# The last convolution's products: half of the row pairs as 64x32, half as pairs of 32x32 spread over two steps, with loads in small pieces

## The chip, the cores and the metric

The kernel runs on one core of one Trainium2 chip, in one launch. The metric is the device time in microseconds; shown are the median and the range of three runs, and one further execution taken with the profiler, from which all rows and durations come. Names: PE is TensorE (matmuls), PEld its weight loads, DVE VectorE, ACT ScalarE, POOL GpSimd, SP SyncE, which only issues transfers.

## What is computed

The reference is a chain of four layers on an image batch `x` of shape 8 x 16 x 256 x 256 (images, channels, rows, columns), all in float32. Each layer normalises its input by groups of two channels and adds its own result to it. The change lies in the last layer. Written with Fourier transforms, it is in effect a 3x3 convolution over 16 channels whose edges wrap around:

```python
def _gn(v, G=8, eps=1e-5):
    B_, C_, H_, W_ = v.shape
    g = v.reshape(B_, G, C_ // G, H_, W_)
    m = jnp.mean(g, axis=(2, 3, 4), keepdims=True)
    s = jnp.var(g, axis=(2, 3, 4), keepdims=True)
    return ((g - m) / jnp.sqrt(s + eps)).reshape(v.shape)

def _L3_conv_ref(x, weight):
    ...
    w_pad = _circular_pad(weight, H, W, k, p)
    dL = jnp.asarray(np.outer(_diag_L(H, k), _diag_L(W, k)))
    Lw = jnp.fft.fft2(w_pad * dL)
    Kx = jnp.fft.ifft2(x, norm='ortho')
    z = jnp.einsum('oihw,bihw->bohw', Lw, Kx)
    y = jnp.fft.fft2(z, norm='ortho')
    return jnp.real(y).astype(x.dtype)

x = x + _L0_conv_ref(_gn(x), L0_conv_weights)
x = x + _L1_conv_ref(_gn(x), ...)
x = x + _L2_conv_ref(_gn(x), ...)
x = x + _L3_conv_ref(_gn(x), L3_conv_weight)
```

## The kernel before

The four layers run one after the other. The last one, `layer3`, starts when layer 2 has written its result to `x3` in device memory, with one column of padding on each side (`WP` = 258 columns).

An image stands in SBUF as a tile of 128 partitions x 33 groups x 258 columns. The 256 rows are cut so that a partition holds one of 8 row positions and one of 16 channels: eight consecutive rows are four "row groups" of two rows, each on 32 partitions. Group index g steps by eight rows. The first image lies in `x30` (named `pt` in the profile, as it shares layer 2's buffer), the others in two tiles `x3s`; three buffers take turns.

An output of two rows x 16 channels, 32 results, needs four input rows, that is two neighbouring row groups of 32 partitions. `products` makes the first half of that sum with q = 0 and the second with q = 1. For each of three column offsets `dw` it issues, for four row pairs j and four column blocks c of the array, a product of a 32 x 32 weight with 512 columns (two groups of 256); so 16 products of 32 rows and 32 columns stand in different cells of the 128 x 128 array. Each product is two matmul instructions in the profile (float32 is made in two passes), each with its own weight load.

A step s = 0 to 3 of an image makes, for each column block c, the 16 output rows of groups 8c + 2s and 8c + 2s + 1: 64 rows. Two steps form a pair and share an output tile `y3` (four buffers). Within a pair the order is: q = 0 of both steps, then q = 1 of both. In PSUM each step has two tiles of two banks; there are four such tiles in all[...]. Between q = 0 and q = 1 a small copy (`seen`, line 1585) reads one column of the banks, by ScalarE for the first step and by VectorE for the second, so that the second half starts only when the first is complete. After q = 1, `evict` adds the bias and writes to `y3`: ScalarE (line 1537) for the even step, VectorE (line 1535) for the odd one, two instructions each. `store` (line 1545) writes the pair with 16 transfers, half on SP's queue and half on POOL's.

Loads: `fetch3` brings an image with two transfers of 16 groups and one of the last group. In `layer3` they are issued by ScalarE: images 1 and 2 at the start, image n + 2 in the middle of image n. `weights` (line 1502) scales the weights by the image's normalisation on VectorE. The normalisation of the last image isn't known when the stage starts; its statistics, a chain of small steps on several engines, are put between the pairs one by one (`todo`).

The order within an engine is the order of the code, since the stage runs under a manual schedule. Earlier, layer 1 (line 1006) uses products of 128 x 32 and of 64 x 32.

Of the kernel before, what the change touches and what calls it, by code (L numbers as in the profile page):

```python
# [10 lines left out]
F32 = mybir.dt.float32  # L11
AF = mybir.ActivationFunctionType
ALU = mybir.AluOpType
# [4 lines left out]
B, C, H, W = 8, 16, 256, 256  # L18
# [96 lines left out]

def _turned(a):

    return np.concatenate([a.reshape(P, 3 * 2 * 32), a[..., ::-1].reshape(P, 3 * 2 * 32)], 1)


def _embedding():
# [162 lines left out]
class _Net:  # L284
# [950 lines left out]
    def stats3_steps(self, pool, name, bank):  # L1235

        nc = self.nc
        mv = self.st3[1]
        e, own, dg, out, nm, bias = (
            pool.tile([P, n], F32, name=f"{name}_{k}")  # L1240
            for k, n in dict(e3=P, own=2, dg=16, bc=16, nm=8, bias=8).items()
        )
        dg, out = dg.rearrange("p (i b) -> p i b", i=2), out.rearrange("p (i b) -> p i b", i=2)
        p, q, u, z = bank(), bank(), bank(), bank()
        (m, r), steps = self.norm_steps(pool, name, bank, self.k["pair"], own[:, 0:1], own[:, 1:2])

        def about():

            nc.vector.tensor_tensor(e, mv[:, 0], p()[:, :P], ALU.subtract)
            nc.vector.tensor_tensor(e, e, e, ALU.mult)  # L1250
            nc.vector.tensor_tensor(e, e, mv[:, 1], ALU.add)

        def columns():
            for i, a in enumerate((mv[:, 0], e)):
                nc.tensor.matmul(q()[:, i : i + 1], a, self.k["mean"][:, 0:1], start=True, stop=True)  # L1255

        def turn():
            nc.vector.tensor_scalar(dg[:, 0], self.k["hi8"], m, None, ALU.mult)
            nc.vector.tensor_scalar(dg[:, 1], self.k["hi8"], r, None, ALU.mult)

        def shift():

            nc.vector.tensor_copy(out, u()[:, :16].rearrange("p (i b) -> p i b", i=2))
            nc.vector.tensor_tensor(nm, out[:, 0], out[:, 1], ALU.mult)
            nc.vector.tensor_scalar(nm, nm, -1.0, None, ALU.mult)

        def sums():

            for q in range(4):
                at = slice(32 * q, 32 * q + 32)  # L1270
                for k in range(6):
                    nc.tensor.matmul(  # L1272
                        z()[at, :8], self.w3[at, 0, k // 2, k % 2], nm[at], start=k == 0, stop=k == 5
                    )
# [34 lines left out]
    def early3(self, pool):  # L1309

        self.st3 = pool.tile([P, P, 6], F32, name="st3"), pool.tile([P, 2, P], F32, name="mv3")
        self.nc.vector.memset(self.st3[1], 0.0)
        self.w3 = pool.tile([P, 2, 3, 2, 32], F32, name="w3")
        self.nc.sync.dma_start(out=self.w3.rearrange("p f d t m -> p (f d t m)"), in_=self.d["l3"])
        self.small = pool

    def patch(self, b, half, c, n):
# [77 lines left out]

    def first3(self, b):

        self.fetch3(self.nc.sync, b, self.x30.rearrange("p (g w) -> p g w", w=WP))

    def stats3(self, bank, name):  # L1400
        out, steps = self.stats3_steps(self.small, name, bank)
# [61 lines left out]

    def fetch3(self, engine, b, xs):

        rows = self.x3[b].rearrange("r c h k w -> (r c) (h k w)")
        at = xs.rearrange("p g w -> p (g w)")
        for k in range(0, 32 * WP, 16 * WP):  # L1470
            engine.dma_start(out=at[:, k : k + 16 * WP], in_=rows[:, k : k + 16 * WP])
        engine.dma_start(out=at[:32, 32 * WP :], in_=rows[:32, :WP])

    def layer3(self, images=range(B)):

# [5 lines left out]
        with ExitStack() as st:  # L1481
# [11 lines left out]

                return get

            def fetch(b, xs):
                self.fetch3(nc.scalar, b, xs)
                return xs

            def weights(b):  # L1500
                ws = io.tile([P, 2, 3, 2, 32], F32, name="ws3")
                nc.vector.scalar_tensor_tensor(  # L1502
                    ws.rearrange("p f d t m -> p (f d t m)"),
                    self.w3.rearrange("p f d t m -> p (f d t m)"),
                    stat[b][0][:, 1, b : b + 1],
                    self.k["ident3"],
                    ALU.mult,
                    ALU.add,
                )
                return ws  # L1510

            def products(s, q, ws, xs, ps):

                for dw in range(3):
                    for j in range(4):
                        k = (j + q) % 4
                        for c in range(4):
                            g = 8 * c + 2 * s + (j + q) // 4
                            nc.tensor.matmul(  # L1519
                                ps[j // 2][32 * c : 32 * c + 32, j % 2].rearrange("p (g w) -> p g w", w=W),  # L1520
                                ws[32 * k : 32 * k + 32, j % 2, dw, q],
                                xs[32 * k : 32 * k + 32, g : g + 2, dw : dw + W],
                                start=q == 0 and dw == 0,
                                stop=q == 1 and dw == 2,
                                skip_group_check=True,
                            )

            def evict(b, s, ps, y):

                bias = stat[b][1][:, b : b + 1]  # L1530
                for k in range(2):
                    src = ps[k].rearrange("p j (g w) -> p g j w", w=W)
                    to = y[:, s % 2, :, 2 * k : 2 * k + 2]
                    if s % 2:
                        nc.vector.tensor_scalar(to, src, bias, None, ALU.add)  # L1535
                    else:
                        nc.scalar.activation(to, src, AF.Identity, bias=bias)  # L1537

            def store(b, s, y):

# [20 lines left out]
                        put(0, [[W, 1], [1, W]], y[0, :, c, 15:16])  # L1561

            images = list(images)
            seen = [io.tile([P, 2, 2], F32, name=f"seen{k}", bufs=1) for k in range(2)]
            xs = [self.x30.rearrange("p (g w) -> p g w", w=WP)]
            ws = weights(images[0])

            stat[images[-1]], todo = self.stats3_steps(self.small, "g3b", bank)
            with tc.manual_schedule():
                for b in images[1:3]:  # L1570
                    xs.append(fetch(b, io.tile([P, 33, WP], F32, name="x3s")))
                for n, b in enumerate(images):
                    for s in (0, 2):
                        y = io.tile([P, 2, 2, 4, W], F32, name="y3", bufs=4)
                        if s and n and n + 2 < len(images):
                            xs.append(fetch(images[n + 2], xs[n - 1]))
                        ps = [[psum.tile([P, 2, 512], F32, name="p3") for _ in range(2)] for _ in range(2)]
                        for q in range(2):
                            for k in range(2):
                                products(s + k, q, ws, xs[n], ps[k])  # L1580
                                if q:
                                    evict(b, s + k, ps[k], y)
                                else:
                                    for h in range(2):
                                        (nc.vector.tensor_copy if k else nc.scalar.copy)(
                                            seen[k][:, h], ps[k][h][:, :, 0]
                                        )
                        store(b, s, y)
                        if todo:
                            todo.pop(0)[2]()  # L1590
                        while todo and todo[0][0] != "PE":
                            todo.pop(0)[2]()
                        if s == 0 and n + 1 < len(images):
                            ws_after = weights(images[n + 1])
                    if n + 1 < len(images):
                        ws = ws_after


@with_exitstack
# [66 lines left out]
```

## Time and profile before

| what | value |
|---|---|
| median of 3 runs | 6728.88 us (6724.0 to 6730.53) |
| the profiled execution's own time | 6725.06 us |
| its span, first to last instruction | 6723.2 us |
| mean granted TensorE clock | 0.985 |
| PE busy over the span | 6116.5 us (91%) |
| last convolution, first to last matmul (line 1519) | about 6444.6 to 6706.9 us from the start |
| of the whole span, matmul records of line 1519 | 6144 of 46024 |

A row of the profile that describes a group of instructions reads: line, engine, operation, output <- inputs by the program's names, shapes, count | busy us, mean ns of one | idle time of the engine just before them, and what ended it. "Issue" there is time in which an engine waited for nothing that the profile shows. A table by stretches gives, for each stretch in us from the start, busy time and count for each engine, then the granted clock, the share of time in which the 16 DMA engines were busy, and what they moved in GB/s. In a timeline the first two numbers are the start and the length in us. A line of a DMA view gives queue and kind, packets, MB and the share of 16 engines' time.

### The profile page before, as it was taken

Reading aid. Unit: us, or ns where it says so; the run is one execution under the profiler, and the core shown is the slowest. Engines: PE = TensorE matmul, PEld = TensorE weight load, DVE = VectorE, ACT = ScalarE, POOL = GpSimd, SP = SyncE. Lnnn points to the kernel's source line nnn. Section 1 sums busy time; section 2 is a strip of 40 time slices with the busy share of each in tenths; the row PEclk is TensorE's granted clock in tenths of the full one; section 3 lists DMA queues with packets and bytes.
Section 4 is the critical chain, followed back from the end, with each engine's and each line's share of the span. In section 5 each row is a group of like instructions: output and inputs, shape, how many; then the busy total and the mean of one; then the engine's idle time right before and its main releaser. Section 6 shows DMA issues by size and latency. Waiting matters only on the chain. (4 is left out here: it accounts for less than half of the span.)

```text
span 6723.2 us, 111466 instructions
## 1 busy us (share of the span) xinstructions
PE 6116.5 (91%) x46024; PEld 2770.6 (41%) x46024; DVE 5401.4 (80%) x6374; ACT 2738.3 (41%) x3898; POOL 3275.4 (49%) x2181
## 2 busy tenths in 40 slices
PE   3898998899899998998997799999999999999987
PEld 1333333333333333333332344444444566666654
DVE  5799999999999999999998899999999633333321
ACT  1333333333333333333332688888888421111211
POOL 0566666666666666666667333444343211111112
PEclk9999999999999999999997899999999999999999
DMA  6233333333333333333332555555556633344256
GB/s 260 61 87 91 92 91 93 88 88 94 90 90 89 88 88 88 88 88 88 88 89 60 180 176 176 175 173 178 176 175 178 174 93 80 80 102 97 81 181 213
DMA packets 372111, 800.86 MB, mean 119 GB/s; under 512 B 56210, under 2 KB 189842, under 8 KB 334354
## 3 DMA queue, kind: packets, MB, share of 16 engines
q1 hardware_dynamic: 329058, 713.30, 36.9%
q10 hardware_dynamic: 36144, 63.64, 2.6%
q0 software_dynamic: 6400, 16.78, 0.9%
q8 instruction: 361, 5.91, 0.4%
q14 instruction: 148, 1.21, 0.1%
HBM read 582.87 MB, written 210.77 MB: 118 GB/s over the span
## 5 line engine op out<-in xcount | busy, mean ns | idle before, releaser
L750 POOL TENSOR_TENSOR dd<-dd 128x1024 f32<-128x1024 f32 x512 | 1214.2, 2372 | 614.8 <-DVE dd L741 594.7
L1006 PE MATMUL ps<-bases,tw 128*32 128x512 f32 (+1 forms) x13824 | 1361.5, 545 | 16.9 <-POOL bases L975 6.5
L741 DVE SCALAR_TENSOR_TENSOR dd<-rb,v 128x1024 f32<-128x1024 f32 (+1 forms) x1024 | 1066.7, 1083 | 97.9 <-PE rb L730 90.2
L975 POOL TENSOR_TENSOR bases<-e,a 128x1024 f32<-128x1024 f32 (+1 forms) x264 | 621.8, 2379 | 928.3 <-DVE e L973 928.0
L629 DVE TENSOR_TENSOR pr<-v,fb 128x2048 f32<-128x2048 f32 (+1 forms) x512 | 1011.5, 2017 | 24.0 <-PE pl L639 12.8
L523 PE MATMUL cv<-kt,w 128*128 128x512 f32 x2048 | 1003.4, 612 | 27.4 <-DVE dd L741 21.4
L532 ACT COPY v<-cv 128x1024 f32<-128x1024 f32 x512 | 517.3, 1010 | 1154.2 <-PE cv L527 1154.2
L1006 PEld LDWEIGHTS ps<-bases,tw 128*32 128x32 f32 x13824 | 599.0, 109 | 800.8 <-issue 483.2
L750 POOL TENSOR_TENSOR s<-s,dd 128x512 f32<-128x512 f32 x512 | 671.3, 1311 | 35.1
L730 PE MATMUL rb<-rs,ct_fold 32*128 32x512 f32 x3584 | 608.7, 649 | 72.1 <-ACT rs L712 68.0
L750 POOL TENSOR_TENSOR s<-v,dd 128x512 f32<-128x512 f32 x256 | 330.7, 1292 | 660.0 <-DVE dd L741 660.0
L639 PE MATMUL pl<-pr,ct_fold 128*32 128x512 f32 x3584 | 532.5, 607 | 117.4 <-DVE pr L629 117.4
L527 PE MATMUL cv<-kt,w 64*128 64x512 f32 x2048 | 578.8, 641 | 0.0
L523 PEld LDWEIGHTS cv<-kt,w 128*128 128x128 f32 x2048 | 354.9, 191 | 524.7 <-issue 299.8
L1430 ACT ACTIVATE vt<-pv,w_b2v 128x128 f32<-128x128 f32 x512 | 146.5, 368 | 842.3 <-PE pv L1426 842.3
L1419 PE MATMUL pqk<-w_qk,t 128*128 128x512 f32 x1024 | 482.7, 594 | 4.6 <-POOL t L1413 4.6
L1451 DVE TENSOR_TENSOR y<-po,res 128x512 f32<-128x512 f32 x128 | 88.5, 692 | 490.9 <-PE po L1446 471.9
L983 DVE SCALAR_TENSOR_TENSOR bases<-xr,xm,bases 128x1024 f32<-128x1024 f32 (+1 forms) x264 | 447.8, 1734 | 0.3 <-POOL bases L975 0.3
L1413 POOL TENSOR_TENSOR t<-t,emb 128x512 f32<-128x512 f32 x128 | 162.3, 1268 | 507.1 <-DVE t L1409 496.4
L960 ACT ACTIVATE sq<-a 128x1024 f32<-128x1024 f32 (+1 forms) x264 | 263.8, 999 | 230.1 <-DVE a L952 229.3
L730 PEld LDWEIGHTS rb<-rs,ct_fold 32*128 32x128 f32 x3584 | 172.8, 185 | 416.3 <-issue 217.7
L942 ACT ACTIVATE d<-xr,bd,sd 128x1024 f32<-128x1024 f32 (+1 forms) x264 | 319.1, 1209 | 14.4 <-DMA xr<-x1p 14.4
(258 smaller groups left out, 8419.4 us busy)
## 6 DMA issues: line engine op xcount, KB each, us to landing
kt<-d SPq DMA_DIRECT2D x256, 516.0 KB
xr<-x1p SPq DMA_DIRECT2D x120, 1024.0 KB
d<-dn ACTq DMA_DIRECT2D x64, 516.0 KB
x<-y SPq DMA_DIRECT2D x128, 258.0 KB
xs<-in_x_dram SPq DMA_DIRECT2D x16, 2048.0 KB
xs<-in_x_dram SPq DMA_DIRECT2D x64, 512.0 KB
res<-in_x_dram SPq DMA_DIRECT2D x64, 512.0 KB
x<-s SPq DMA_DIRECT2D x128, 256.0 KB
```

Source lines behind the costliest of these rows:

```text
L523: nc.tensor.matmul(ps()[:, n], w[:, 0, j, :], t[:, a : a + 2, 0:W], start=True, stop=False)
L527: nc.tensor.matmul(ps()[:, n], w[at, 1, j, :], t[at, a : a + 2, 2 - n : 2 - n + W], start=False, stop=True)
L532: nc.scalar.copy(v[h]()[:, 4 * g : 4 * g + 4, j * W : j * W + W], ps().rearrange("p n (a w) -> p (n a) w", w=W),)
L629: nc.vector.tensor_tensor(pr()[:, :n].rearrange("p n (r w) -> p n r w", w=W), v[h]()[:, 4 * g : 4 * g + n].rearrange("p n (r w) -> p n r w ...
L639: nc.tensor.matmul(pl()[at : at + 32], sel[:, g, h, :], pr()[:, t, :], start=h == 0 and g == 0, stop=h == 1 and (g == 1 or t == 3),)
L730: nc.tensor.matmul(r()[:, n], spread[at, g, h, :], rs()[at], start=True, stop=True)
L741: nc.vector.scalar_tensor_tensor(dd()[:, :n], r()[:, :n], 1.0 / B, v[h]()[:, a : a + n], ALU.subtract, ALU.mult)
L750: op("POOL", us, lambda: nc.gpsimd.tensor_tensor(out[0](), a[0](), b[0](), ALU.add), a[1] + b[1], out[1])
L975: nc.gpsimd.tensor_tensor(ring[n % 3][:, 0, p : p + m, 1 : 1 + W], rows(e), rows(a), ALU.subtract)
L983: nc.vector.scalar_tensor_tensor(r, rows(part[1]), xm[:, b : b + 1], v, ALU.is_gt, ALU.mult)
L1006: nc.tensor.matmul(out if k is None else out[:, k], lhs, rhs, start=start, stop=stop, skip_group_check=True)
L1419: nc.tensor.matmul(ps, t[:, n, k * P : (k + 1) * P], wqk[:, n, :], start=n == 0, stop=n == 1)
```

## The change

- Even row pairs (`whole`): the two row groups of output pair j = 0 or 2 are neighbours that start at partition 0 or 64, so both halves of the sum are made at once, as one product with a 64 x 32 weight. A step has 3 x 2 x 4 = 24 of them.
- Odd row pairs (`halves`): as before in two halves of 32 x 32. The q = 0 half of a step is issued together with the q = 1 half of the step before it; the two use different rows of the array and different PSUM tiles. A step has 2 x 24 = 48 of them, and a last call after the loop makes the last q = 1 half.
- PSUM: a step has one tile for its even and one for its odd pairs. The even tile is evicted by ScalarE in its own step, the odd one by VectorE in the next. The stores of a pair of steps are issued one step later than the pair's end. One `seen` copy a step, by ScalarE.
- Loads: nine transfers an image (eight of four groups, one of the last group), on SP and POOL in turn, behind the stores of these queues: image 1 at the start, and image n + 2 in two portions, after steps 1 and 3 of image n.
- The weights are laid out anew: 96 columns for the 64-row products and 192 for the halves, 288 for 384.

```diff
+    both = np.concatenate([np.stack([a[2 * h + q, :, :, :, q] for q in range(2)]) for h in range(2)])
+    return np.concatenate([both.reshape(P, 3 * 32), a[..., ::-1].reshape(P, 3 * 2 * 32)], 1)
...
-    def fetch3(self, engine, b, xs):
+    def fetch3(self, engines, b, xs, part=range(9)):
 
         rows = self.x3[b].rearrange("r c h k w -> (r c) (h k w)")
         at = xs.rearrange("p g w -> p (g w)")
-        for k in range(0, 32 * WP, 16 * WP):
-            engine.dma_start(out=at[:, k : k + 16 * WP], in_=rows[:, k : k + 16 * WP])
-        engine.dma_start(out=at[:32, 32 * WP :], in_=rows[:32, :WP])
+        n = 4 * WP
+        for i in part:
+            engine = engines[i % len(engines)]
+            if i < 8:
+                engine.dma_start(out=at[:, i * n : (i + 1) * n], in_=rows[:, i * n : (i + 1) * n])
+            else:
+                engine.dma_start(out=at[:32, 32 * WP :], in_=rows[:32, :WP])
...
+            def product(ps, j, c, rows, w, xs, g, dw, start, stop):
+                nc.tensor.matmul(
+                    ps[32 * c : 32 * c + 32, j].rearrange("p (g w) -> p g w", w=W),
+                    w[rows],
+                    xs[rows, g : g + 2, dw : dw + W],
...
+            def whole(s, ws, xs, ps):
 
                 for dw in range(3):
-                    for j in range(4):
-                        k = (j + q) % 4
+                    for j in range(2):
                         for c in range(4):
...
+                            rows = slice(64 * j, 64 * j + 64)
+                            product(ps, j, c, rows, ws[0][:, dw], xs, 8 * c + 2 * s, dw, dw == 0, dw == 2)
+
+            def halves(work):
+
+                for dw in range(3):
+                    for q, s, ws, xs, ps in work:
+                        for j in range(2):
+                            k = (2 * j + 1 + q) % 4
+                            rows = slice(32 * k, 32 * k + 32)
+                            for c in range(4):
+                                g = 8 * c + 2 * s + (2 * j + 1 + q) // 4
+                                product(
+                                    ps, j, c, rows, ws[1][:, dw, q], xs, g, dw, q == 0 and dw == 0, q == 1 and dw == 2
+                                )
+
+            def evict(b, s, j, ps, y):
...
+                to = y[:, s % 2, :, j::2]
+                if j:
+                    nc.vector.tensor_scalar(to, src, bias, None, ALU.add)
+                else:
+                    nc.scalar.activation(to, src, AF.Identity, bias=bias)
...
+                    full, part = (psum.tile([P, 2, 512], F32, name="p3") for _ in range(2))
+                    whole(s, ws, xs[n], full)
+                    evict(b, s, 0, full, y)
+                    now = (b, s, part, y)
+                    work = [(0, s, ws, xs[n], part)]
+                    if before:
+                        work.append((1, *before[0]))
+                    halves(work)
+                    nc.scalar.copy(seen, part[:, :, 0])
+                    if before:
+                        self.done(evict, store, *before[1])
+                    before = (s, ws, xs[n], part), now
+                    if s % 2:
+                        if n + 2 < len(images):
+                            self.fetch3(loads, images[n + 2], xs[n + 2], range(4, 9) if s > 1 else range(4))
...
+                halves([(1, *before[0])])
+                self.done(evict, store, *before[1])
+
+    @staticmethod
+    def done(evict, store, b, s, ps, y):
+        evict(b, s, 1, ps, y)
+        if s % 2:
+            store(b, s - 1, y)
```

`loads` is `[nc.sync, nc.gpsimd]`. What remains of the step's end (the statistics' steps, the weights of the next image) stands where it stood, after every odd step.

More of the change, by code (lines that the diff above doesn't have):

```diff
@@ L116, in _turned @@
 def _turned(a):
-    return np.concatenate([a.reshape(P, 3 * 2 * 32), a[..., ::-1].reshape(P, 3 * 2 * 32)], 1)
+    both = np.concatenate([np.stack([a[2 * h + q, :, :, :, q] for q in range(2)]) for h in range(2)])
+    return np.concatenate([both.reshape(P, 3 * 32), a[..., ::-1].reshape(P, 3 * 2 * 32)], 1)
 def _embedding():
@@ L1272, in sums @@
                     nc.tensor.matmul(
-                        z()[at, :8], self.w3[at, 0, k // 2, k % 2], nm[at], start=k == 0, stop=k == 5
+                        z()[at, :8], self.w3[at, 96 + 32 * k : 128 + 32 * k], nm[at], start=k == 0, stop=k == 5
                     )
@@ L1312, in early3 @@
         self.nc.vector.memset(self.st3[1], 0.0)
-        self.w3 = pool.tile([P, 2, 3, 2, 32], F32, name="w3")
-        self.nc.sync.dma_start(out=self.w3.rearrange("p f d t m -> p (f d t m)"), in_=self.d["l3"])
+        self.w3 = pool.tile([P, 288], F32, name="w3")
+        self.nc.sync.dma_start(out=self.w3, in_=self.d["l3"])
         self.small = pool
@@ L1396, in first3 @@
     def first3(self, b):
-        self.fetch3(self.nc.sync, b, self.x30.rearrange("p (g w) -> p g w", w=WP))
+        self.fetch3([self.nc.sync], b, self.x30.rearrange("p (g w) -> p g w", w=WP))
     def stats3(self, bank, name):
@@ L1494, in bank @@
                 return get
-            def fetch(b, xs):
-                self.fetch3(nc.scalar, b, xs)
-                return xs
+            loads = [nc.sync, nc.gpsimd]
             def weights(b):
-                ws = io.tile([P, 2, 3, 2, 32], F32, name="ws3")
+                ws = io.tile([P, 288], F32, name="ws3")
                 nc.vector.scalar_tensor_tensor(
[L1503 to L1508, printed above, removed]
-                )
-                return ws
@@ L1512, in products @@
-            def products(s, q, ws, xs, ps):
+                    ws, self.w3, stat[b][0][:, 1, b : b + 1], self.k["ident3"], ALU.mult, ALU.add
+                )
+                return ws[:, :96].rearrange("p (d m) -> p d m", d=3), ws[:, 96:].rearrange(
+                    "p (d t m) -> p d t m", d=3, t=2
+                )
[4 more added lines that the diff above has]
+                    xs[rows, g : g + 2, dw : dw + W],
+                    start=start,
+                    stop=stop,
+                    skip_group_check=True,
+                )
@@ L1514, in products @@
+            def whole(s, ws, xs, ps):
                 for dw in range(3):
-                    for j in range(4):
-                        k = (j + q) % 4
+                    for j in range(2):
                         for c in range(4):
[L1518 to L1526, printed above, removed]
@@ L1528, in evict @@
-            def evict(b, s, ps, y):
-                bias = stat[b][1][:, b : b + 1]
[L1531 to L1537, printed above, removed]
+                            rows = slice(64 * j, 64 * j + 64)
@@ new lines, in whole @@
+                            product(ps, j, c, rows, ws[0][:, dw], xs, 8 * c + 2 * s, dw, dw == 0, dw == 2)
[9 more added lines that the diff above has]
+                                    ps, j, c, rows, ws[1][:, dw, q], xs, g, dw, q == 0 and dw == 0, q == 1 and dw == 2
+                                )
@@ L1539, in store @@
+            def evict(b, s, j, ps, y):
+                bias = stat[b][1][:, b : b + 1]
+                src = ps.rearrange("p j (g w) -> p g j w", w=W)
+                to = y[:, s % 2, :, j::2]
[3 more added lines that the diff above has]
+                    nc.scalar.activation(to, src, AF.Identity, bias=bias)
             def store(b, s, y):
@@ L1563, in layer3 @@
             images = list(images)
-            seen = [io.tile([P, 2, 2], F32, name=f"seen{k}", bufs=1) for k in range(2)]
+            seen = io.tile([P, 2], F32, name="seen", bufs=1)
             xs = [self.x30.rearrange("p (g w) -> p g w", w=WP)]
@@ L1569, in layer3 @@
             with tc.manual_schedule():
[L1570 to L1573, printed above, removed]
-                        y = io.tile([P, 2, 2, 4, W], F32, name="y3", bufs=4)
[L1575 to L1588, printed above, removed]
+                for b in images[1:2]:
+                    xs.append(io.tile([P, 33, WP], F32, name="x3s"))
+                    self.fetch3(loads, b, xs[1])
@@ new lines, in layer3 @@
+                steps = [(n, b, s) for n, b in enumerate(images) for s in range(4)]
+                before = None
+                for n, b, s in steps:
+                    if s == 0 and n + 2 < len(images):
+                        xs.append(xs[n - 1] if n else io.tile([P, 33, WP], F32, name="x3s"))
+                    if s % 2 == 0:
+                        y = io.tile([P, 2, 2, 4, W], F32, name="y3", bufs=4)
+                    full, part = (psum.tile([P, 2, 512], F32, name="p3") for _ in range(2))
[13 more added lines that the diff above has]
+                            self.fetch3(loads, images[n + 2], xs[n + 2], range(4, 9) if s > 1 else range(4))
@@ L1592, in layer3 @@
                             todo.pop(0)[2]()
-                        if s == 0 and n + 1 < len(images):
-                            ws_after = weights(images[n + 1])
-                    if n + 1 < len(images):
+                    if s == 1 and n + 1 < len(images):
+                        ws_after = weights(images[n + 1])
+                    if s == 3 and n + 1 < len(images):
                         ws = ws_after
+                halves([(1, *before[0])])
[5 more added lines that the diff above has]
+            store(b, s - 1, y)
 @with_exitstack
```

## The prediction

> **What bounds the kernel now.** I read the page's head first, then a table by stretches, because only the last convolution (line 1519) changes and the shares of the whole span say nothing about it.
>
> ```profile
> span 6723.2 us, 111466 instructions
> ...
> core 0: us, PE busy (x) PEld busy (x) DVE busy (x) ACT busy (x) POOL busy (x), PEclk, DMA share, GB/s
> 6650.93:6660.06 9.13, 9.13 (x302) 6.51 (x292) 2.79 (x4) 0.32 (x2) 3.71 (x7) 1.00 0.55 146
> 6444.60:6706.90 262.30, 231.34 (x6204) 132.48 (x6204) 49.46 (x89) 42.12 (x68) 51.96 (x97) 0.95 0.70 237
> 6448.00:6464.00 16.00, 12.78 (x335) 7.12 (x319) 1.60 (x3) 2.44 (x4) 0.00 (x0) 0.91 1.01 424
> 6656.00:6660.00 4.00, 4.00 (x140) 2.95 (x126) 0.32 (x2) 0.00 (x0) 1.86 (x4) 1.00 0.98 272
> 6706.90:6723.20 16.30, 0.00 (x0) 0.00 (x0) 2.01 (x2) 0.00 (x0) 3.71 (x7) 0.60 0.45 129
> ```
>
> The stage takes 262.3 us of TensorE and 16.3 us of last eviction and stores. VectorE and ScalarE are busy for 49 and 42 us of it, so neither bounds it. In an undisturbed stretch (first row) three calls of `products` take 9.13 us: 3.04 us a call, and the other clean calls lie between 2.8 and 3.2; I take 3.07. The 64 calls would then need 196 us. Where are the other 66? The groups and the chain of waits, taken in order of time, say it:
>
> ```profile
> L1519 PE MATMUL p<-x3s,ws 32*32 32x512 f32 x3840 | 141.9, 617 | 19.3 <-issue 19.2
> L1519 PE MATMUL p<-pt,ws 32*32 32x512 f32 x2304 | 87.5, 646 | 17.7 <-issue 11.5 <-DVE ws L1502 6.1
> ...
> 6595.59 4.49 PE p L1519 x124
> 6600.07 2.82 issue
> 6602.90 6.09 PE p L1519 x125
> 6608.98 1.77 issue
> ...
> q10 hardware_dynamic: 169, 2.53, 102.7%
> q8 instruction: 1, 0.02, 1.0%
> ```
>
> 6144 matmul records are 3072 products in two passes each. TensorE stops for "issue", no other engine, about every 124 matmuls, that is every 250 of its instructions (each has a weight load). The last two lines are the DMA view of 6598 to 6604 us: the load queue fills all 16 engines, and queue 8 moves one packet of instructions. Read packet by packet, queue 8 brings 16384 bytes each time, and TensorE goes on 2.2 to 2.5 us after such a packet starts. 24 stops of 0.6 to 3.4 us stand beside such packets: 45 us. They are longest under the image loads (2 to 3.4), 0.6 to 2.1 under stores, none while the DMA engines idle. The remaining 21 us are the statistics' matmuls (about 5) and some 24 us at half clock (mean 0.95): about 11 lost, with 5 unexplained.
>
> So two things bound the stage: 3.07 us a call, and instructions that arrive late.
>
> **The change, part by part.** *The 64x32 products.* Per step (two calls, 6.14 us clean) there were 96 products of 32x32; there are now 24 of 64x32 and 48 of 32x32: 144 matmul records for 192. The array is no freer, as 64x32 occupies two cells. The trace has this very shape in layer 1, 48 records of 512 columns over 8 tiles, between other modes:
>
> ```profile
> 4244.44 0.86 PE L1006 MATMUL ps<-bases,tw 128*32 128x512 f32 x5
> ...
> 4245.22 2.81 PE L1006 MATMUL ps<-silu,wm 64*32 64x512 f32 x48
> ...
> 4247.96 1.07 PE L1006 MATMUL ps<-bases,tw 128*32 128x512 f32 x8
> ```
>
> From its first start to the first of the next mode: 2.74 us, six rounds of 8 at 0.43 us. That is `whole`, with the switch out of its mode. `halves` keeps 96 records on 16 tiles, as one call now: 3.07 us, first two rounds perhaps at 0.43 us instead of 0.51, as after a stop; I keep 3.07 plus 0.03 for the entry.[...] The row: the last round before the switch takes 0.52 us for 0.43, 0.1 dearer. With 64 switches the row costs 6 us (already inside 2.74 and 3.10)[...]. The first and last `halves` have one part only, 2.6 us each (48 records, 8 tiles, like the row). Sum: 32 x 2.74 + 31 x 3.10 + 2 x 2.6 = 189 us for 196. Only 7 us: fewer instructions alone bring little[...].
>
> *Instruction blocks.* 32 x 144 x 2 = 9216 instructions plus a few: 36 blocks of 16 KB for 48. A block of 256 lasted 4.1 us at 16.0 ns each (3.07 us over 192); now 5.2 us (5.84 us over 288), so each arrival has 1.1 us more. Taking 1.1 us off every stop leaves 20 of the 45 us; with 36 blocks for 48, 15. Against that, the DMA engines, idle for a third of the stage, will be nearly always busy, so more blocks meet traffic; for it, the image loads come in rows of 4128 bytes for 16512, so a block waits behind shorter packets. Bounds: 4 and 45 us. I take 18, near the scaled row.[...]
>
> *Loads.* They move from ScalarE's queue (3 DMAs an image) to SP and POOL in turn (9 an image), behind the stores of the previous pair there. ScalarE gains 3 issues, off the path: nothing. POOL pays 541 ns each (its row of stores), SP about 0.6 to 2 each; per pair SP then issues 8 stores and 2 or 3 loads, some 8 to 11 us of 11.7, and nothing but later stores stands behind them. A load waits only for buffers that are free since the image's first step and is used four steps later, some 24 us: its cost is nothing while that lead lasts.[...] The pieces here are 528 KB[...]. The rows have stores of 256 KB overlapping at 272 GB/s, so I take no fixed cost.
>
> *Bandwidth.* A pair of steps moves 2.1 MB in and 2.1 MB out in 11.7 us plus about 1.1 of stops: 328 GB/s. Loads alone run at 424, stores alone at 272: half and half 331. That just fits, for six of the eight images; what lags is stored later, as there are four `y3` buffers, and the last two images only store. Cost 0, at worst 15.
>
> *Evictions, seen, waits.* One 1.11 us eviction on ScalarE and one 1.28 on VectorE per step, as many as now; one `seen` copy of 0.16. Part of step s is finished by step s+1's `halves`; VectorE then needs about 0.6 + 1.28 us, and TensorE needs the bank again after `whole`, 2.74 us later: covered by 0.9. If ScalarE stands waiting for a `y3` buffer, `seen` stands behind it, and the next `halves` waits: only when stores lag by three pairs. `weights` shrinks from 384 to 288 columns, 0.61 us, covered except the first: -0.1. At the end VectorE evicts once, not twice: -1.3.
>
> *Sum.* 189 + stops 18 + statistics 5 + half clock and rest 10 (fewer long stops, but a cold start on fuller rounds) = 222 for 262.3, -40; with the end -41.6. The profiled execution's 6725.06 becomes 6683.5; the median of the runs shown is 3.8 above that execution: 6687, say 6686.
>
> **The rivals.** *A, the instructions stay the bound* (0.14): the blocks wait as long as now because the engines are always busy; stops stay 45 us, -14 us: 6714. For it: most stops fall where DMA is full. Against: 1.1 us more per block. *B, the array is the bound and the blocks come in time* (0.16): `halves` at 2.83, stops 4, clock 5: 8 + 14 + 5 better than my sum, 6659. For it: first rounds after a stop do run at 0.43 us. Against: later rounds fall back to 0.51 and more. *C, slower: DMA becomes the bound* (0.05): 64.5 MB in 283 us now; when loads share the rings of the stores in small rows the mixture could fall below 231 GB/s, from where on the stage is longer than today; at 215 it is 300 us, 17 more: 6746. Against: even stores alone reach 272 in full stretches. *D, the change does not bring its concurrency*: the two parts in one `halves` use other rows and banks, so they should run together; if they did not, 3 rounds more a step would cost 1.3 us x 32, +42 minus the gain, 6729; 0.02.
>
> **How the numbers follow.** My forecast has a chance of 0.63, B 0.16, A 0.14, C 0.05, D 0.02. About 0.2%, 13.4 us, is what a measurement of this kernel can tell from no change. My case and B lie wholly under 6715; of A half (0.07); the other half of A, D and a share of C (0.01) are no change: faster 0.86, same 0.10, slower 0.04. The range runs from 6656 (B and a little more) to 6714 (stops unchanged).
>
> **What would show it.** In the profile after: 64*32 rows, 1536 records in groups of 48 at 2.7 us; 32*32 rows 3072; a step pair near 12 us clean; fewer "issue" stops than 24 and shorter ones; 36 packets on queue 8; DMA share 0.85 to 0.95 until image 6; no load queue 10. I am wrong if a group of 48 takes over 3 us, if `halves` takes much over 3.2, if "issue" stays 45 us, or if evictions wait for stores by tens of us.

## The result, and the profile after

| | before | after |
|---|---|---|
| median of 4 runs | 6726.94 us (6724.0 to 6730.53) | 6689.96 us (6685.81 to 6690.8) |
| ratio | | 0.9942 (95%: 0.993 to 0.9954) |
| the profiled execution's own time | 6725.06 us | 6685.81 us |
| last convolution, first to last matmul | 262.2 us | 221.9 us |
| after the last matmul | 16.3 us | 12.9 us |

The kernel is 37 us faster. The profiled executions differ by 39.3 us, and three terms make that up: the stage is 40.3 shorter, the end 3.4 shorter, and the stage starts 4.5 later. The late start is none of the change's: the drift arises in layer 0, and the start lay anywhere from 6447 to 6457 us in the runs below.

The page's head and the table by stretches, as for before: an undisturbed stretch of three steps, the stage, a stretch under loads, the end.

```profile
span 6684.0 us, 108481 instructions
...
core 0: us, PE busy (x) PEld busy (x) DVE busy (x) ACT busy (x) POOL busy (x), PEclk, DMA share, GB/s
6639.98:6658.23 18.25, 18.25 (x441) 6.77 (x433) 3.85 (x3) 3.83 (x6) 5.92 (x12) 1.00 0.73 208
6449.17:6671.10 221.93, 215.02 (x4668) 77.55 (x4668) 45.64 (x57) 43.78 (x68) 67.36 (x125) 0.99 0.85 277
6453.40:6469.30 15.90, 15.90 (x346) 5.64 (x338) 2.50 (x5) 3.83 (x6) 0.00 (x0) 1.00 0.82 329
6671.10:6684.00 12.90, 0.00 (x0) 0.00 (x0) 1.28 (x1) 0.00 (x0) 3.68 (x7) 0.62 0.64 197
```

TensorE idles for 7 us of the stage (221.93 - 215.02), where it idled for 31. The clock is 0.99 for 0.95, and the DMA engines are busy for 0.85 of the time for 0.70. In the stretch under loads TensorE is busy without a gap for 15.9 us while 329 GB/s flow; before, it was busy for 12.8 of 16.0 us, at 424 GB/s. (The like stretch at 424 GB/s stands below, with e1.) The first row gives the clean step: 18.25 / 3 = 6.08 us.

In the groups by form the records are as many as planned (960 + 576 of 64 rows, 1920 + 1152 of 32), and the idle time ahead of them, 37 us before, is 12.9:

```profile
L1513 PE MATMUL p<-x3s,ws 32*32 32x512 f32 x1920 | 81.5, 598 | 2.6 <-issue 2.5 <-ACT seen L1602 0.2
L1513 PE MATMUL p<-x3s,ws 64*32 64x512 f32 x960 | 61.2, 608 | 2.6 <-issue 2.6
L1513 PE MATMUL p<-pt,ws 32*32 32x512 f32 x1152 | 54.0, 598 | 1.3 <-issue 1.3
L1513 PE MATMUL p<-pt,ws 64*32 64x512 f32 x576 | 35.8, 615 | 6.4 <-DVE ws L1505 6.0 <-issue 0.4
```

Of these 12.9, 6.0 are one wait for the first image's weights, as before; no idle time of TensorE is put down to a store, and `seen` costs 0.2. The clean step is read from the timeline of weight loads, where a mode's first load has its own row (start, length):

```profile
6649.39 0.18 PEld L1513 LDWEIGHTS p<-x3s,ws 64*32 64x32 f32 x16 [0.84 <-issue]
...
6652.16 0.26 PEld L1513 LDWEIGHTS p<-x3s,ws 32*32 32x32 f32 x32 [0.84 <-issue]
...
6655.49 0.18 PEld L1513 LDWEIGHTS p<-x3s,ws 64*32 64x32 f32 x16 [0.84 <-issue]
...
6658.23 0.29 PEld L1513 LDWEIGHTS p<-x3s,ws 32*32 32x32 f32 x32 [0.84 <-issue]
```

6655.49 to 6658.23 is `whole`, 2.74 us, and nearly every step shows just that. 6652.16 to 6655.49 is `halves`, 3.33 us; 3.34 is the usual value where no stop falls into it.

The chain of waits over the stage and the DMA view of the stage (queue and kind, packets, MB, share of 16 engines):

```profile
by line: PE p L1513 95.0%; issue 3.1%; DVE y L1549 0.6%; PE p L1273 0.5%; PE p L1256 0.2%; DVE ws L1505 0.2%; PE p L1278 0.2%; PE p L1287 0.1%; PE p L1197 0.1%; PE p L1199 0.1%; ACT seen L1602 0.1%; DVEq L1549 0.0%; ACTq L1602 0.0%
...
q0 software_dynamic: 10432, 31.58, 44.7%
q1 hardware_dynamic: 14608, 31.81, 38.2%
q8 instruction: 37, 0.61, 1.0%
```

The line of queue 8 in the same view of before:

```profile
q8 instruction: 49, 0.80, 1.1%
```

"Issue" is 3.1% of the chain; in the same view of before it was 13.8%. I count a stop where the gap between two matmul starts is over 0.57 us and ends 1.9 to 2.9 us after a packet of queue 8 starts, and take 0.45 us, a usual gap, off each. Before then has 23 stops with 34.0 us in sum, after 10 with 8.1. Time at half clock within the stage fell from 26.6 us to 6.5, of which 3.1 lie at its start. Queue 8 brings 37 packets of instructions for 49, of 16384 bytes each, and the old load queue is gone from the view. With 9336 PE and PEld records in the stage (12408 before) that is 252 a packet (253 before); I put a block at 256 instructions, an estimate from these counts.

### The profile page after: what moved, and what is told of

It is laid out like the page before. It is cut to its first block, busy times and chain, and to the rows that moved or that the text cites. A ratio compares the mean times of both kernels' runs of the same rounds, so it can differ in the third digit from the quotient of the medians.

```text
span 6684.0 us, 108481 instructions
## 1 busy us (share of the span) xinstructions
PE 6103.0 (91%) x44488; PEld 2715.6 (41%) x44488; DVE 5395.8 (81%) x6342; ACT 2739.9 (41%) x3898; POOL 3291.4 (49%) x2209
## 5 line engine op out<-in xcount | busy, mean ns | idle before, releaser
L630 DVE TENSOR_TENSOR pr<-v,fb 128x2048 f32<-128x2048 f32 (+1 forms) x512 | 1011.6, 2017 | 24.1 <-PE pl L640 12.8
```

The lines of the kernel that those rows point to most:

```text
L630: nc.vector.tensor_tensor(pr()[:, :n].rearrange("p n (r w) -> p n r w", w=W), v[h]()[:, 4 * g : 4 * g + n].rearrange("p n (r w) -> p n r w ...
```

## The experiments

My theory when they began: (a) the clean step is shorter with the 64-row products; (b) stops are shorter because a block of 256 instructions lasts longer; (c) the short rows of the new loads let a block through sooner. The rivals: that the loads alone bring the gain; that refilling is merely slower than the pace of the instructions, traffic or not; that the two parts of `halves` do not run together; that the DMA engines limit the clean step. All stage lengths are from the first to the last matmul, each from one profile; a ratio is to the runs of before on the same chip (medians 6728.79 us for e1 to e4, 6726.94 for e5 to e8, 6729.93 for e10 to e13).

| kernel | stage, us | stops: number, us | median, us | ratio to before (95%) |
|---|---|---|---|---|
| before | 262.2 | 23, 34.0 | 6726.94 | |
| after | 221.9 | 10, 8.1 | 6689.96 | 0.9942 (0.993 to 0.9954) |
| e12_after_again | 221.2 | 9, 8.4 | 6688.83 | 0.9942 (0.9927 to 0.9956) |
| e1_old_loads | 217.7 | 10, 8.0 | 6683.75 | 0.9933 (0.9917 to 0.995) |
| e2_new_loads | 260.7 | 26, 37.4 | 6739.58 | 1.0015 (1.0006 to 1.0023) |
| e3_after_no_loads | 203.6 | 3, 0.8 | 6671.86 | 0.9916 (0.9901 to 0.9931) |
| e4_before_no_loads | 228.6 | 15, 12.5 | 6697.12 | 0.9954 (0.9939 to 0.9969) |
| e5_apart | 246.7 | 4, 1.0 | 6711.52, one run | |
| e6_rows_first | 218.5 | 12, 7.0 | 6683.11 | 0.9932 (0.9915 to 0.9948) |
| e7_16_groups | 220.4 | 9, 10.2 | 6687.88 | 0.994 (0.9925 to 0.9955) |
| e8_act_queue | 218.8 | 6, 6.2 | 6687.89 | 0.9941 (0.9926 to 0.9956) |
| e10_before_no_traffic | 213.8 | 2, 3.3 | 6684.0, one run | |
| e11_after_no_traffic | 201.4 | 0, 0 | 6664.97, one run | |
| e13_both | 216.4 | 10, 5.7 | 6686.74 | 0.9942 (0.9925 to 0.9958) |

**The two halves of the change, one at a time.** First the new products with the old loads: three transfers an image, issued by ScalarE.

```diff
-                    self.fetch3(loads, b, xs[1])
+                    self.fetch3([nc.scalar], b, xs[-1])
...
+                    if s == 2 and n and n + 2 < len(images):
+                        self.fetch3([nc.scalar], images[n + 2], xs[n + 2])
...
-        n = 4 * WP
+        n = 16 * WP
```

> The products of the changed kernel with the loads of the kernel before (two pieces of 16 groups and one of the last group, on ScalarE's queue, images 1 and 2 at the start, image n + 2 in the middle of image n). My theory (both parts matter: fewer instruction blocks with more time for each, and short rows ahead of them): stops for instructions between those of the two kernels, about 20 to 25 us against 45 and 11, stage about 232 us against 222, in all about 6700. Rival 1 (the loads alone bring the gain): stops near 45 us, in all about 6722. Rival 2 (the products alone bring it): stops near 11 us, in all about 6690.

Then the old products with the new loads, on SP and POOL in portions behind each pair's stores:

```diff
-                    xs.append(fetch(b, io.tile([P, 33, WP], F32, name="x3s")))
+                    self.fetch3(loads, b, xs[1])
...
                         store(b, s, y)
+                        if n + 2 < len(images):
+                            self.fetch3(loads, images[n + 2], xs[n + 2], range(4, 9) if s else range(4))
```

> The products of the kernel before with the loads of the changed kernel (nine small pieces on SP and POOL, in two portions an image). My theory: 48 blocks of instructions with the short time of before, but shorter rows ahead of them: stops about 30 us, in all about 6712. Rival 1 (the loads alone bring the gain): about 6690. Rival 2 (the products alone): 6727, stops near 45 us.

The two stages, e1 and then e2, in the table by stretches:

```profile
6451.50:6669.20 217.70, 211.04 (x4668) 75.76 (x4668) 45.65 (x57) 43.73 (x68) 51.93 (x97) 0.98 0.82 282
```

```profile
6453.10:6713.80 260.70, 227.05 (x6204) 129.90 (x6204) 49.70 (x89) 41.88 (x68) 67.07 (x125) 0.97 0.77 238
```

The products alone bring the whole gain, and the loads alone none: 260.7 us is before's stage within 2 us, with 26 stops for 23 (37.4 us for 34.0), and the time is even 0.15% longer. (The profile of e2 is of an execution of 6729.70 us, 10 us under its median, so where that 0.15% arises is not shown.)

e1 also allows the comparison of like with like: its loads are those of before. At the same distance from the stage's start as before's load stretch, and at the same 424 GB/s, TensorE is busy for 16.00 us of 16.00, where it was busy for 12.78:

```profile
6454.90:6470.90 16.00, 16.00 (x358) 5.68 (x342) 2.50 (x5) 3.66 (x5) 0.00 (x0) 1.00 1.01 424
```

e2's chain shows the old stops under the new loads:

```profile
6595.42 4.49 PE p L1521 x120
6599.91 3.37 issue
6603.28 18.67 PE p L1521 x473
6621.95 1.93 issue
```

So (c) fell: a stop of 3.37 us stands under loads in rows of 4128 bytes, as one of 2.82 did under rows of 16512.

**Without loads.** After with images 2 to 7 not loaded (earlier tiles are used again), and before likewise:

```diff
-                        xs.append(xs[n - 1] if n else io.tile([P, 33, WP], F32, name="x3s"))
+                        xs.append(xs[n])
...
-                            self.fetch3(loads, images[n + 2], xs[n + 2], range(4, 9) if s > 1 else range(4))
```

> The changed kernel without the loads of images 2 to 7: all images from 1 on are computed from image 1's data, so the output of the later images is another. My theory: the traffic of loads is what delays the remaining stops; 11 us of stops fall to 0 to 3, stage about 211 us, in all about 6677, and a clean step stays at 6.07 us[...]. Rival (bandwidth holds back evictions and so the products): the clean step gets shorter and the stage falls under 205 us.

> The kernel before without the loads of images 2 to 7 (images 0 and 1 take turns as input, so the output of the later images is another). My theory: the stops under loads go, those under stores stay: about 18 of 45 us remain, stage about 235 us, in all about 6700. Rival (the stops come from the number of instructions, not from traffic): stops stay near 45 us, in all about 6725.

```profile
6452.60:6656.30 203.70, 203.05 (x4668) 75.33 (x4668) 45.65 (x57) 43.65 (x68) 54.02 (x101) 0.99 0.60 176
```

```profile
6450.40:6679.00 228.60, 218.13 (x6204) 133.78 (x6204) 49.13 (x89) 42.09 (x68) 51.93 (x97) 0.99 0.56 160
```

Loads cost after 18.3 us (221.9 - 203.6) and before 33.6 (262.2 - 228.6). In e3 the clean step is still 2.74 + 3.34, so the DMA engines do not limit it, and that rival fell. But e3's stage went below what I expected, since loads cost more than the stops that I count: 18.3 us for 7.3 us of stops (where the rest lies is said below, with what stays open). In e4 one stop stays in each pair of steps, under the stores (12.94 us is two steps of two calls each):

```profile
6610.00 0.77 issue
6610.77 12.94 PE p L1519 x355
6623.70 0.22 issue
6623.93 12.94 PE p L1519 x356
6636.86 0.22 issue
```

**Without any traffic.** This was to settle whether a block is late because of traffic or because of the pace. Both kernels, with neither the loads of images 2 to 7 (left out as in e3 and e4) nor the stores of images 0 to 6:

```diff
 # before
-                        store(b, s, y)
+                        if b == images[-1]:
+                            store(b, s, y)
 # after
-        if s % 2:
+        if s % 2 and b == B - 1:
             store(b, s - 1, y)
```

> The kernel before without the loads of images 2 to 7 and without the stores of images 0 to 6 (images 0 and 1 take turns as input; most of the output is not written). Without loads it still stopped once a pair of steps, 0.8 to 1.4 us, under stores alone. If traffic is what delays the blocks of instructions, these stops go in images 1 to 6: a pair of steps takes 12.3 us (6.17 a step), the stage about 208 us. If the pace is what does it (a block of 256 instructions is used up in about 4.1 us, sooner than the next can come even from idle engines), the stop in every pair stays, a pair takes 13.2 us or more, the stage about 220 to 228 us.

> The changed kernel without the loads of images 2 to 7 and without the stores of images 0 to 6 (images from 1 on computed from image 1's data; most of the output is not written). The floor of the new products: 32 steps of 6.07 us, the statistics and the cold start, 203 to 204 us for the stage as in the run without loads, if stores cost TensorE nothing; 200 us or less if evictions that wait for stores cost something.

```profile
6454.70:6668.50 213.80, 210.74 (x6204) 148.04 (x6204) 48.79 (x89) 41.99 (x68) 3.39 (x6) 0.99 0.10 34
```

```profile
6449.20:6650.50 201.30, 201.13 (x4668) 75.25 (x4668) 45.66 (x57) 43.65 (x68) 5.39 (x10) 0.99 0.10 33
```

And e10 from 6480 to 6660 us in the table by stretches, and its chain from 6590 to 6650 us, which in before is cut about every 124 matmuls:

```profile
6480.00:6660.00 180.00, 180.00 (x5387) 130.03 (x5360) 44.05 (x76) 37.11 (x60) 2.96 (x6) 1.00 0.03 7
...
by line: PE p L1519 100.1%
...
6589.98 60.04 PE p L1519 x1685
```

With the same instructions at the same pace and the DMA engines idle but for 7 GB/s, TensorE is busy for 180.00 us on end. Two stops are left, and both stand beside traffic that this run keeps: one at 6466 us, just behind the load of image 1, and one at 6666, with the last image's stores. The pace rival, which wanted a stage of 220 to 228 us, fell: it is 213.8. My own figure, 208, was also too low; the old calls last 3.17, 3.21, 3.14 and 3.19 us here, 6.36 a step, not twice the 3.07 that I had read in before. A call that follows a stop is shorter (2.85 us behind before's stop that ends at 6661.78 us), and I had averaged such calls in.

These two runs split the gain. Without traffic the new products are 12.4 us faster (213.8 - 201.4; e10's two stops, 3.3 us, are in it); the other 27.9 us of the 40.3 are traffic that hurts less: 48.4 us in before (262.2 - 213.8), 20.5 in after (221.9 - 201.4).

**The two parts of `halves`, one behind the other.** Same instructions, loads and stores; only the order changes.

```diff
-                    work = [(0, s, ws, xs[n], part)]
+                    halves([(0, s, ws, xs[n], part)])
                     if before:
-                        work.append((1, *before[0]))
-                    halves(work)
+                        halves([(1, *before[0])])
```

> The changed kernel, but the two parts that share a call of halves (first halves of this step, second halves of the step before) are issued one after the other, each on 8 tiles. My theory: the gain needs both on 16 tiles at once. Each part alone takes 2.6 to 2.74 us (six rounds of 0.43), so a step becomes 2.74 + 5.3 = 8.1 us for 6.07, the stage about 285 us, in all about 6750; no stops are left, as a block of instructions now lasts 7.2 us. Rival (halves is bound by the number of instructions, 17 ns each): two parts of 48 records take 3.34 us together as before and the stage stays near 222 us.

```profile
6449.90:6696.60 246.70, 246.47 (x4668) 93.67 (x4668) 45.64 (x57) 43.68 (x68) 67.09 (x125) 0.99 0.79 250
```

The timeline of its weight loads, again at the first one of each mode:

```profile
6644.49 0.18 PEld L1513 LDWEIGHTS p<-pt,ws 32*32 32x32 f32 x16 [0.84 <-issue]
...
6649.21 0.18 PEld L1513 LDWEIGHTS p<-pt,ws 64*32 64x32 f32 x16 [0.84 <-issue]
...
6651.95 0.18 PEld L1513 LDWEIGHTS p<-pt,ws 32*32 32x32 f32 x16 [0.84 <-issue]
```

`halves` takes 4.72 us for 3.34, so the two parts do run together in after, and that is worth 1.38 us a step. It was expected at 5.3 and a stage of 285, but the end of one part runs beside the start of the next: in this trace groups of eight matmuls start 0.43 us apart within a part, and 0.23 us apart where the two parts meet. The second reading is worth more. The step is now 4.72 + 2.74 = 7.46 us with the same 288 instructions and the same loads and stores, so a block lasts 256 / 288 x 7.46 = 6.6 us, and the stops are 1.0 us where after has 8.1. A longer stage also spreads the traffic, 250 GB/s for 277; but e2, with the same loads at 238 GB/s and blocks of 4.2 us, has 37.4 us of stops. So in these runs the time that a block lasts decides the stops, and (b) stands. Even so slowed, the kernel took 15 us less than before in its one run.

**Why `halves` takes 3.34 us.** The column block c, innermost in after, is moved outward, so that successive weight loads go to different rows of the array:

```diff
                 for dw in range(3):
-                    for q, s, ws, xs, ps in work:
-                        for j in range(2):
...
-                            for c in range(4):
+                    for c in range(4):
+                        for q, s, ws, xs, ps in work:
+                            for j in range(2):
```

> The changed kernel with another order within halves: for each column block the four row groups follow each other, instead of four column blocks on the same row group. Theory 1[...]: halves stays at 3.34 us and the stage near 222 us. Theory 2 (a weight load has to wait for matmuls that run on the same row group): halves falls towards 2.75 us, the stage to about 204 us, in all about 6671.

```profile
6649.31 0.29 PEld L1513 LDWEIGHTS p<-x3s,ws 32*32 32x32 f32 x32 [0.84 <-issue]
...
6652.65 0.18 PEld L1513 LDWEIGHTS p<-x3s,ws 64*32 64x32 f32 x16 [0.84 <-issue]
...
6655.39 0.29 PEld L1513 LDWEIGHTS p<-x3s,ws 32*32 32x32 f32 x32 [0.84 <-issue]
```

3.34 us again: the order of the weight loads is not the cause, and that theory fell.

**Size and queue of the loads.** Sixteen groups a transfer on SP and POOL (e7), four groups a transfer on ScalarE's queue (e8), and after unchanged once more (e12), to see how far two runs of one kernel lie apart:

```diff
 # e7
-        n = 4 * WP
+        n = 16 * WP
...
 # e8
-            loads = [nc.sync, nc.gpsimd]
+            loads = [nc.scalar]
```

> The changed kernel with loads in pieces of 16 groups (rows of 16512 bytes) as before, but still on SP and POOL and in two portions. If the size of the rows matters for the wait of instruction blocks, as the prediction had it, stops rise from 8 to about 20 us and the whole to about 6700. If it does not, as the run with the old loads suggests, the stage is 218 to 224 us and the whole 6684 to 6692.

> The changed kernel with its nine small loads an image on ScalarE's queue, in the same two portions. If the queue matters (on SP and POOL the loads stand behind stores and share their rings), the stage falls to that of the run with the old loads, about 218 us, in all about 6684. If not, it stays at 222 us and 6690. ScalarE's nine issues an image, 0.3 to 1.3 us each, could also hold back its evictions: then some steps grow by a wait for the PSUM tile, and the whole is over 6695.

> The changed kernel once more, on the same chip as the next run. Tells how much of the 4 us between its stage (221.9 us) and those of the variants with other loads (217.7 to 220.4) is chance: a stage of 218 to 222 us is expected, in all about 6687 to 6690.

On the same queues the size makes 220.4 for 221.9 and 221.2 us, nothing that one profile each can separate. The stages with ScalarE's queue (217.7, 218.8, and 216.4 below) are 2.4 to 5.5 us shorter than those of after, but e6 reached 218.5 on SP and POOL, and the intervals of all the ratios overlap. That ScalarE's queue is better remains a hint.

**A version with both.** e1's loads and e6's order together:

> The new products with the old loads (large, on ScalarE's queue) and the order with row groups first: the two variants that came out lowest, together. If their 4 us are real and add up, the stage is 214 us and the whole about 6680; if they are chance, 217 to 222 us and 6683 to 6690.

```profile
6448.80:6665.20 216.40, 211.83 (x4668) 76.16 (x4668) 45.64 (x57) 43.77 (x68) 51.91 (x97) 0.99 0.83 284
```

The shortest stage of the full kernels, and yet 6686.74 us in the median, between after and e1. No version is shown to beat after.

## Why the prediction was right, and where it was not

The forecast was 6686 and the median is 6690; the stage was put at 222 us and took 221.9. The mechanism held, but an agreement within 0.1 us in the stage is luck: two errors cancel. With the steps as measured the products take 32 x 2.74 + 31 x 3.34 + 2 x 2.6 = 196.4 us, 7.4 more than the 189 of the sum. What e11 has beyond them, 5.0 us (201.4 - 196.4), is about the 5 put for the statistics, though a slow start is in it (the first 235 matmuls of e11's chain take 13.17 us, later stretches of 278 take 12.14). Traffic then adds 20.5 us (221.9 - 201.4), where stops, half clock and rest had been put at 28: 7.5 less.

- `whole`, 2.74 us from layer 1's rows: exact. With a switch of mode on either side, `whole` still takes 2.74 us in after.
- `halves`, put at 3.10: the mis-sized term. It takes 3.34, so the sum has 0.24 x 31 = 7.4 us too little. The step behind it, "`halves` keeps 96 records on 16 tiles, as one call now: 3.07 us", was sound in kind, but 3.07 was an average with calls that follow a stop. Without traffic the old call is 3.18 (e10), and `halves` is 0.16 above even that.
- Before's clean calls were too low by the same error, 6.14 us a step for 6.36. So the clean gain, put at 7 us, is 9 by these steps ((6.36 - 6.08) x 32), and 12.4 between the whole stages of e10 and e11, of which 3.3 are e10's two stops.
- Stops, put at 18: 8.1, or 13 without the 0.45 us that is taken off each. In the way that the prediction counted, before's 45 stand against these 13. The mechanism was right and both halves of it are shown: traffic makes the blocks late (without it, 180 us of e10 pass with no stop), and the longer block absorbs it (e1 is busy for 16.00 us of 16.00 where before was for 12.78, under the same 424 GB/s; and e5 has 1.0 us of stops for 8.1). By this count the size was too high: the scaled row, 15, was near, and the 3 us that I put on top for busier DMA engines were not needed, though these are busy for 0.85 of the stage. Measured against e11, late blocks cost about 19 us (below); by that measure the 18 was near, and it is the 10 for half clock and rest that was too much. The clean blocks last 256 / 384 x 6.36 = 4.2 us and 256 / 288 x 6.08 = 5.4, so the lead is 1.2 us and not 1.1.
- Under traffic before stops at the distance of a block (124 and 125 matmuls apart in its chain from 6595 us); how many blocks lie ready at a time was not measured.
- The short rows of the new loads, counted in favour of the change, bring nothing (e2, e7). Nor do the small loads show a cost of their own: after's trace has 277 GB/s over the stage, and e7's four times larger pieces save at most 1.5 us.
- Half clock and rest, put at 10: 6.5 us at half clock are left, some 3 us lost (the 3.4 us at 6609 lengthen one `whole` by 1.7).
- The end, put at 1.3 shorter: 3.4 shorter. The prediction counted the one eviction saved on VectorE, and gave no gain to the last stores; what made the rest shorter was not tried.
- Two of the prediction's own signs of being wrong came up. `halves` takes more than 3.2 us, as said. And evictions do wait for stores by tens of us, 46.2 in after's view of waits (us in total, times, longest), for 25.5 in before's:

```profile
DVE y L1549 <- DMA out_dram<-y: 26.0, 5, 5.7
ACT y L1551 <- DMA out_dram<-y: 20.2, 7, 3.3
```

```profile
ACT y L1537 <- DMA out_dram<-y: 18.0, 3, 6.2
DVE y L1535 <- DMA out_dram<-y: 7.5, 1, 7.5
```

  In the groups by form these waits do not reach TensorE: 0.2 us for `seen`, nothing for an eviction or a store. The way by which they were to cost time, through `seen`, was named rightly; its cost of about nothing held.
- Rival A (stops stay 45) and D (no concurrency) are refuted by after's own profile and by e5. D's sum was also too small: by the prediction's own row two parts of six rounds at 0.43 us take 5.2 us, 2.1 more a step and not 1.3. That its 1.3 is near e5's 1.38 is luck: there the two parts overlap for a while. B wanted `halves` at 2.83, and C a DMA below 231 GB/s; measured were 3.34 and 277.

What stays open: why `halves` takes 3.34 us and not six rounds at 0.43 plus the entry. Its rounds on 16 tiles take 0.56 us on average where `whole` has 0.43 on 8. What is excluded is the order of the weight loads (e6) and the DMA traffic (e3, and e11, where it is 3.34 us as well); what sets it, no run here shows.

The part of traffic's 20.5 us that the 8.1 us of stops leave out can be found by laying after's 64 stretches between two changes of mode beside the same stretches of e11. 22 are longer, by 20.5 us in sum. One of them, 1.7 us longer, lies at half clock and holds one of the ten counted stops; e1 has one just as long at half clock, with no block arriving in it. The other 21, together 18.8 us, each have a block arriving in them (put at 2.3 us after a packet of queue 8 starts; at the ten counted stops TensorE goes on 2.2 to 2.6 us after one): 14.2 us in the nine with a counted stop, 4.6 in twelve without one. (Of the 42 stretches that are not longer 18 have an arrival too: those blocks came in time.) So late blocks cost after about 19 us. The count of 8.1 is too low, as it takes 0.45 us off each stop and leaves out shorter delays.

## What to carry to other kernels

Where TensorE idles for "issue" at a regular distance in instructions, beside full DMA engines, ask whether it is waiting for its own program, as it was here (stops about every 124 matmuls, each ending 1.9 to 2.9 us after a packet of queue 8 starts), and lay the packets of the instruction queue beside the stops. The remedy here was fewer instructions for the same work, so that each block lasts longer (5.4 us for 4.2), and not other transfers (e2's stage is 260.7 us, before's 262.2). A duration for a clean call is read only from calls with no stop just ahead of them: in e4 those behind a stop take 2.80 us, in e10's steady stream a call takes 3.14 to 3.21.

## What the runs showed that I had not expected

- The larger part of what fewer instructions bring is not their own time: 12.4 us without traffic, 40.3 with it.
- Stores alone also delay the instruction blocks: in e4, with no loads, before loses 14.8 us to them (228.6 - 213.8), after 2.2 (203.6 - 201.4). The counted stops are 12.5 us in e4 and 3.3 in e10.
- A round of 16 tiles of 32 x 32 does the same work as a round of 8 tiles of 64 x 32 (16 x 32 x 32 = 8 x 64 x 32), yet the first takes 0.53 us (3.18 / 6, e10's calls) and the second 0.43.
